# A GNN's first layer taken by chunks, with two of sixteen tiles' source rows by one-hot products from an on-chip table

## The chip, the cores and the metric

The kernel runs on one core of a Trainium2 chip. The core's engines work side by side: TensorE (PE; its weight loads are listed apart as PEld), VectorE (DVE), ScalarE (ACT), GpSimd (POOL) and SyncE (SP), with DMA queues that these engines issue to. The time is that of the device for one execution, in microseconds (us); the smaller, the better. Beside it stands one execution recorded by the profiler, whose span runs from the first to the last recorded event.

## The reference

A graph has N = 12,500 nodes with 32 features each and E = 400,000 edges, sorted by their target node `dst`; the source nodes `src` are random. Four layers follow each other, each on `h = relu(layernorm(x))`, and each adds its result to `x`:

```python
# layer 0
m = relu(h[src] + edge_attr_32)
x = x + (1 + eps) * h + segment_sum(m, dst)
# layer 1: messages from h[src], h[dst] and a 3-vector of the edge, with weights
#          made from edge_attr_10 by a small network; segment_sum over dst
# layer 2: norm * (segment_sum((norm * h)[dst], src) + norm * h), norm = rsqrt(1 + degree of src)
# layer 3: messages from h[src], edge_attr_4 and a network on edge_attr_8; segment_sum over dst
```

Layer 0 is the one whose loop is rewritten. Per edge it fetches a row of 32 numbers by `src`, adds the edge's own 32 numbers, applies relu and sums the result into the row of `dst`. The degree of each node as a source, which layer 2 needs, is counted in the same loop.

## The kernel before

Edges are taken in tiles of 128 (one edge per partition), 3136 tiles in all; 16 tiles are a chunk (196 chunks of 2048 edges) and 4 tiles a group, so a chunk has 4 groups. As `dst` is sorted, the targets of a chunk usually fall into a window of 128 consecutive nodes. `setup()` and `windows()` run ahead of the layers. `setup()` writes zeros to ten tables of 1.56 MB that collect the sums (`acc`, on ACT's DMA queue, L281), loads and scales the weights of the later layers (L126 to L187), and loads `x`. `windows()` loads `dst` (L203), works out each edge's place in its chunk's window (L214) and stores the places for later (`local`, L218; `loc_t`, L225, in another order), decides by a flag (L251) whether all windows fit, and then normalizes the edges' 3-vectors for layer 1 in two orders (L257 to L277, with `rsqrt`, L291 to L296). The flag is read into a register and chooses between two programs; the profile is that of the one for fitting windows, called fast here.

`layer0()` starts with the layer norm of `x` (L309 on), which writes `feat0`, the table of rows that edges fetch. Then `edges()` (L440) runs over chunks and groups. It fetches four groups ahead: on SP the chunk's `src` (L395), its `edge_attr` (L393) and its places (`local`, L376), and on POOL one indirect DMA per tile (L401), which gathers 128 rows of `feat0` by 128 indices into a buffer `hs`. There are six such buffers of one group each (`gather0`), and two of each chunk load (`big0`).

Per group, `main` adds the edge attributes on DVE (L523, 128x128) and applies relu on ACT (L524). `tail`, one group later, calls `collect`: DVE makes four one-hot matrices of the places (L350, 128x512) and TensorE multiplies them with the messages (L353, the one-hot as the weights, 32 columns moving, f32), accumulating the chunk's window in PSUM. After the last group ACT copies the window (`wsum`, L356) and SP writes it to one of two tables in turn (L366). Also in `tail` is the degree: the source number is split into `hi` and `lo` (L538 to L541), both become bf16 one-hots (L545) and TensorE multiplies them (L548); DVE adds the chunk's histogram to the sum (L551).

Nothing orders the work but the program order on each engine, the queues, and the number of buffers in each pool. After the loop the two tables are loaded and added to `x` (`gather_sum`, `part<-acc`). Layers 1 and 2 are fused, layer 3 follows; neither is touched.

Of the kernel before, what the change touches and what calls it, by code (L numbers as in the profile page):

```python
# [8 lines left out]
F32 = mybir.dt.float32  # L9
# [8 lines left out]
D = 32  # L18
# [8 lines left out]
NTAB = 4  # L27
ROUND = 12582912.0
# [7 lines left out]
class GNN:  # L36
# [14 lines left out]
    def __init__(self, tc, ctx, a, out, E):  # L51
# [15 lines left out]

        self.mid = dram.tile([rows, D + 1], F32, name="mid", tag="mid")
# [10 lines left out]
    def setup(self):  # L79
# [18 lines left out]
        once = ExitStack()  # L98
        pool = once.enter_context(self.tc.tile_pool(name="once", bufs=1))
# [9 lines left out]
        nc.vector.tensor_scalar_mul(self.minus, self.part, -1.0)  # L109
        self.eye = keep.tile([P, P], F32, name="eye")  # L110
# [5 lines left out]
        zero = pool.tile([P, J * D], F32, name="zero")  # L116
        nc.vector.memset(zero, 0.0)
        for l in range(4):
            for t in self.tabs[l] if l == 2 else self.tabs[l][:2]:
                self.clear(t, zero)  # L120
            nc.scalar.dma_start(self.feats[l][self.N :], zero[:, :D])
        nc.scalar.dma_start(self.mid[self.N :], zero[:, : D + 1])


        self.w1a = keep.tile([10, 16], F32, name="w1a")
# [4 lines left out]
        self.w2a = keep.tile([16, 896], F32, name="w2a")  # L130
# [8 lines left out]


# [4 lines left out]
        self.w1t = keep.tile([P, P], F32, name="w1tk")  # L145
        nc.vector.tensor_scalar_mul(self.w1t, hid, math.sqrt(2.0) / math.sqrt(10.0))
        lo = pool.tile([P, 6, P], F32, name="wlo")
        hi = pool.tile([P, 4, P], F32, name="whi")
        for r in range(2):
            nc.sync.dma_start(lo[64 * r : 64 * r + 64], self.a["w2lo"])  # L150
            nc.sync.dma_start(hi[64 * r : 64 * r + 64], self.a["w2hi"])
        self.w2t = keep.tile([P, 6, P], F32, name="w2t")
# [5 lines left out]
                                       op0=ALU.mult, op1=ALU.add)  # L158

        mod = pool.tile([P, 8], F32, name="mod")  # L160
        nc.vector.tensor_reduce(mod, self.eye.rearrange("p (k w) -> p w k", w=8), AX.X, ALU.add)
        self.sums = keep.tile([P, 6, D], F32, name="sums")
        nc.vector.memset(self.sums, 0.0)
        for j in range(3):
            nc.vector.tensor_copy(self.sums[:, j, 8 * j : 8 * j + 8], mod)
            nc.vector.tensor_copy(self.sums[:, 3 + j, 0:24].rearrange("p (w i) -> p w i", i=3)[:, :, j], mod)

        self.w1b = keep.tile([8, 256], F32, name="w1b")
        nc.sync.dma_start(self.w1b, self.a["L3_gnn_fc_w1"])
        nc.vector.tensor_scalar_mul(self.w1b, self.w1b, math.sqrt(2.0) / math.sqrt(8.0))  # L170
        self.w1q = keep.tile([P, 256], F32, name="w1q")
# [3 lines left out]
        nc.vector.tensor_scalar_mul(self.w1q, self.w1q, math.sqrt(2.0) / math.sqrt(8.0))  # L175
        rawb = pool.tile([P, 2, 4, 8, 8], F32, name="w2rawb")
        nc.sync.dma_start(rawb.rearrange("p c i w u -> p c (i w u)"),
                          self.a["L3_gnn_fc_w2"].rearrange("(c p) f -> p c f", p=P))
        self.w2b = keep.tile([P, 2, 256], F32, name="w2b")
# [260 lines left out]
    def edges(self, load, gather, front, main, tail, begin=None, windowed=None):  # L440
# [4 lines left out]
        with self.tc.For_i(0, self.T // IT, 1) as it:  # L445
# [22 lines left out]
            for g in range(n):  # L468
# [5 lines left out]
                if g:  # L474
                    tail(*state.pop(g - 1))
# [875 lines left out]
```

## Time and profile before

| what | us |
|---|---|
| median of 3 executions | 23369.61 (23297.51 to 23409.01) |
| the profiled execution, its own time | 23468.87 |
| its span | 23467.2 |
| from the start to the first gather of layer 0 | 388.0 |
| layer 0, first gather to the loading of its tables | 388.0 to 5326.6 |
| layers 1 and 2 | about 5405 to 16,680 |
| layer 3 | about 16,680 to 23,417 |
| POOL's gathers of layer 0 (L401), 3136 of them | 3105.7 busy |

In the page of the profile a row of digits cuts the span into 40 equal slices; a digit is the busy share of an engine in tenths. A group is one line of the source on one engine: the operation, what it writes and reads, its count, then its busy time, the mean duration of one in ns, and how long the engine stood idle just before it, with what ended most of that. "Issue" is idle time that ended by nothing the profile shows; "remote" (in the chain of waits "another core or an unknown queue") is a wait whose releaser the trace could not tie to an instruction of this core. The answers on stretches of time list the busy time and the number of instructions of each engine, the clock that TensorE was granted, the busy share of the DMA engines and the GB/s they moved.

### The profile page before, as it was taken

How to read it: one execution, taken by the hardware profiler on the slowest of the kernel's cores; microseconds unless marked ns; L12 is line 12 of the kernel's file. 1: busy time of each engine (PE TensorE's matmuls, PEld its weight loads, DVE VectorE, ACT ScalarE, POOL GpSimd, SP SyncE). 2: the span in 40 equal slices, each digit the busy share in tenths (PEclk: the TensorE clock that was granted, in tenths of full speed). 3: DMA queues.
4: the chain of work that ended last, by engine and by line, in shares of the span. 5: the costliest groups of instructions: out<-in, count | busy, mean ns of one | idle time of the engine just before them, and what ended most of it. 6: DMA issues, size and time to landing. Idle time of an engine off the chain costs nothing.

```text
span 23467.2 us, 229097 instructions
## 1 busy us (share of the span) xinstructions
PE 15908.4 (68%) x74484; PEld 8469.3 (36%) x74484; DVE 11846.5 (50%) x24268; ACT 5514.0 (23%) x12941; POOL 14360.9 (61%) x12552
## 2 busy tenths in 40 slices
PE   1333333335877787777778777777488888888887
PEld 1333333332333333333333333333254445545444
DVE  4333333334555555555555555556355555555555
ACT  0000000002222222222222222222133333333333
POOL 2666666664777777777777777777444444444443
PEclk9999999998777777777777777777688887788887
DMA  2111111112333333333333333334100000000000
GB/s 97 23 23 22 23 23 23 22 23 64 81 79 80 80 80 78 76 78 80 78 77 82 77 82 77 80 79 80 32 12 12 12 12 12 12 12 12 12 12 18
DMA packets 1486556, 1138.48 MB, mean 49 GB/s; under 512 B 1139620, under 2 KB 1290484, under 8 KB 1430308
## 3 DMA queue, kind: packets, MB, share of 16 engines
q1 hardware_dynamic: 728300, 889.84, 12.3%
q0 software_dynamic: 752640, 206.32, 10.9%
q10 hardware_dynamic: 4398, 27.49, 0.3%
q8 instruction: 591, 9.68, 0.2%
q14 instruction: 627, 5.14, 0.1%
HBM read 1022.56 MB, written 99.86 MB: 48 GB/s over the span
## 4 chain that ended last, share of the span: by engine, by line
PE 38%; DVE 18%; another core or an unknown queue 16%; issue 12%; ACT 9%; POOL 3%; DMA 3%; DVEq 0%; SPq 0%; ACTq 0%; POOLq 0%
PE ps_y L709 10%; PE ps_w L1125 10%; PE ps_o L719 4%; PE ps L842 4%; ACT oh L744 3%; DVE z L712 3%; PE ps_h L1103 2%; DVE pb L1135 2%; ACT oh L673 2%; DVE rb L1143 2%; PE ps_win L353 2%; POOL hs L401 1%; PE ps_sum L1164 1%; DMA hs<-feat,src 1%
## 5 line engine op out<-in xcount | busy, mean ns | idle before, releaser
L848 POOL DMA_INDIRECT acc<-summed,rows x3136 | 4995.2, 1593 | 1969.5 <-issue 1074.5
L1093 POOL DMA_INDIRECT hs<-feat,src x3136 | 3085.5, 984 | 3658.9 <-DVE pb L1135 2663.2
L401 POOL DMA_INDIRECT hs<-feat,src x3136 | 3105.7, 990 | 2196.0 <-issue 873.2
L1125 PE MATMUL ps_w<-w2b,hid 128*128 128x256 f32 x12544 | 4007.2, 462 | 638.0 <-issue 457.3
L667 POOL DMA_INDIRECT hs<-feat,src_c x3136 | 3173.7, 1012 | 1139.1 <-issue 931.3
L353 PE MATMUL ps_win<-m,oh 128*128 128x32 f32 x6272 | 1498.8, 403 | 3077.2 <-ACT m L524 2203.0
L1125 PEld LDWEIGHTS ps_w<-w2b,hid 128*128 128x128 f32 x12544 | 2733.1, 228 | 2327.7 <-issue 1596.3
L712 DVE TENSOR_TENSOR z<-ps_y,hid 128x1024 f32<-128x1024 f32 x2352 | 2843.1, 1218 | 1195.4 <-PE ps_y L709 1006.7
L709 PE MATMUL ps_y<-X,w2t 64*128 64x512 f32 x4704 | 2253.6, 836 | 675.3 <-ACT hid L704 375.8
L353 PEld LDWEIGHTS ps_win<-m,oh 128*128 128x128 f32 x6272 | 1399.8, 328 | 3173.0 <-ACT m L524 2258.9
L1130 DVE TENSOR_TENSOR pa<-ps_w,q 128x512 f32<-128x512 f32 x784 | 540.1, 689 | 3158.9 <-PE ps_w L1125 2902.5
L719 PE MATMUL ps_o<-z,sums 128*32 128x512 f32 x9408 | 1929.8, 695 | 0.9 <-DVE z L712 0.6
L709 PE MATMUL ps_y<-Q,w2t 64*128 64x512 f32 x4704 | 1678.0, 737 | 91.3 <-DVE z L712 40.8
L686 PE MATMUL ps_m<-eye,hs 128*32 128x128 f32 x6272 | 803.1, 367 | 1007.7 <-ACT X L692 780.1
L842 PEld LDWEIGHTS ps<-hd,eq 128*128 128x128 f32 x6272 | 1039.7, 251 | 1229.4 <-issue 324.6
L842 PE MATMUL ps<-hd,eq 128*128 128x32 f32 x6272 | 1135.7, 334 | 508.4 <-DVE eq L834 174.6
L695 DVE TENSOR_TENSOR Q<-N,X 128x512 f32<-128x512 f32 x392 | 272.1, 695 | 2159.7 <-ACT X L692 1359.3
L1105 ACT ACTIVATE hid<-ps_h 128x1024 f32<-128x1024 f32 x784 | 800.1, 1021 | 2177.8 <-PE ps_h L1103 1850.9
L1135 DVE TENSOR_TENSOR pb<-ps_w,hs 128x256 f32<-128x256 f32 x3136 | 1286.5, 476 | 0.0
L709 PEld LDWEIGHTS ps_y<-X,w2t 64*128 64x128 f32 x4704 | 605.5, 238 | 1720.5 <-issue 728.2
L1103 PE MATMUL ps_h<-emb,w1q 8*128 8x512 f32 x3136 | 1067.5, 762 | 228.9 <-DMA emb<-in_ea_c 165.0
L350 DVE TENSOR_TENSOR oh<-iota,local 128x512 f32<-128x512 f32 x784 | 536.9, 685 | 1174.1 <-remote 1033.5
(190 smaller groups left out, 18558.0 us busy)
## 6 DMA issues: line engine op xcount, KB each, us to landing
has<-loc_t SPq DMA_DIRECT2D x392, 1024.0 KB
srow<-in_src_t SPq DMA_DIRECT2D x392, 512.0 KB
hs<-feat,src POOLq DMA_INDIRECT x6272
N<-n_t SPq DMA_DIRECT2D x3136, 32.0 KB
edge_attr<-in_edge_attr SPq DMA_DIRECT2D x196, 256.0 KB
hs<-feat,src_c POOLq DMA_INDIRECT x3136
acc<-summed,rows POOLq DMA_INDIRECT x3136
emb<-in_ea_c SPq DMA_DIRECT2D x784, 20.0 KB
```

Of the source, the lines that this page charges most:

```text
L353: nc.tensor.matmul(c["sum"], lhsT=oh[:, k, :], rhs=feat[:, k, :], start=t0 + k == 0, stop=t0 + k == self.CT - 1)
L401: self.nc.gpsimd.indirect_dma_start(out=t[:, k, :], out_offset=None, in_=self.feats[l][:], in_offset=bass.IndirectOffsetOnAxis(ap=idx[:, t ...
L667: nc.gpsimd.indirect_dma_start(out=c["hs"][:, k, :], out_offset=None, in_=self.feats[1][:], in_offset=bass.IndirectOffsetOnAxis(ap=c["src_ ...
L709: nc.tensor.matmul(y[:, q, :], lhsT=self.w2t[64 * q : 64 * q + 64, j, :], rhs=c["Q" if j < 3 else "X"][64 * q : 64 * q + 64, h, :], start= ...
L712: nc.vector.tensor_mul(z, y, c["hid"][:, 2 * h : 2 * h + 2, :])
L719: nc.tensor.matmul(c["o", j // 3][32 * q : 32 * q + 32, :], lhsT=self.sums[:, j, :], rhs=c["z", j, q // 2][:, q % 2, :], start=j % 3 == 0, ...
L842: nc.tensor.matmul(t[:, k, :], lhsT=c["eq"][:, k, :], rhs=c["hd"][:, G * g + k, :], start=True, stop=True)
L848: nc.gpsimd.indirect_dma_start(out=self.tabs[2][k % NTAB][:], out_offset=bass.IndirectOffsetOnAxis(ap=c["rows"][:, G * g + k : G * g + k + ...
L1093: nc.gpsimd.indirect_dma_start(out=c["hs"][:, k, :], out_offset=None, in_=self.feats[3][:], in_offset=bass.IndirectOffsetOnAxis(ap=c["src" ...
L1103: nc.tensor.matmul(t[:, q, :], lhsT=self.w1q[r : r + 8, m * P : (m + 1) * P], rhs=c["emb"][r : r + 8], start=True, stop=True)
L1125: nc.tensor.matmul(w[:, k, :], lhsT=c["hid"][:, m, 4 * g + k].rearrange("p q s -> p (q s)"), rhs=self.w2b[:, m, :], start=m == 0, stop=m == 1)
L1135: nc.vector.tensor_mul(c["pb"][:, i, gs], w[:, :, lo : lo + 64].rearrange("p g (w u) -> p g w u", u=8), by[:, :, None, :].to_broadcast([P, ...
```

## The change

The loop of layer 0 is replaced for the fast program by `edges0`, which works on whole chunks. Three things differ in it.

First, from the fourth chunk on, POOL gathers only 14 of the 16 tiles. The rows of the last two tiles (256 edges) are looked up on chip. `table` loads `feat0` once as 3157 rows of 4 nodes (the table has 128 spare rows), in 25 blocks of up to 128 such rows, and splits each number into three bf16 parts that add up to it. `codes`, run once, writes for each of the 256 edges of each chunk three numbers: the block, the place in the block and which of the four nodes. SP loads them to all 128 partitions. `found` compares the place with the partition number (`mine`), then for each of 25 blocks makes a bf16 one-hot (DVE, 128x256) and has TensorE multiply three parts of the table with it, 75 products summed in one PSUM tile: column e then holds the four nodes' 128 numbers of edge e's row. A mask keeps the node that is meant (`own`), a product with `fold` turns and sums it, and ACT copies the result beside the gathered rows.

Second, the one-hots of the window sums are made by ACT (16 Square and 4 Relu per chunk, `places`), and `collect` uses the messages as 32-column weights in four column tiles; `add` folds the four parts together one chunk later. The message sum and its relu run once per chunk (128x512), as do the coordinates of the degree.

Third, the setup is shorter: the norm of layer 0 stands ahead of `windows()`, `dst` is loaded on ACT's queue, and clearing tables, the weights, `loc_t` and the normalized vectors move into a generator, `rest`. Two of its steps (the clearing of layer 0's own two tables) are taken ahead of the loop, the others inside it, two per group from the fifth chunk on: 10 clears, 6 for weights, 8 for places, 84 for the vectors, now in 14 blocks. The program for windows that do not fit keeps the old loop (`any0`).

```diff
--- before.py
+++ after.py
+KP = 2
+KB = 25
...
     def setup(self):
...
-        for l in range(4):
-            for t in self.tabs[l] if l == 2 else self.tabs[l][:2]:
-                self.clear(t, zero)
...
+    def weights(self, pool):
...
+    def rest(self, pool):
+        nc, J = self.nc, self.J
+        zero = pool.tile([P, J * D // 8], F32, name="zero")
+        nc.vector.memset(zero, 0.0)
+        for l in range(4):
+            for t in self.tabs[l][:2] if self.fast and l != 2 else self.tabs[l]:
+                self.clear(t, zero)
+                yield
+        yield from self.weights(pool)
+        if self.fast:
+            yield from self.places_by_edge(pool)
+            yield from self.unit_vectors(pool)
...
     def windows(self):
...
-            nc.sync.dma_start(dst.rearrange("p w t -> p (w t)"), self.a["dst"])
+            nc.scalar.dma_start(dst.rearrange("p w t -> p (w t)"), self.a["dst"])
...
-        with self.tc.tile_pool(name="unit", bufs=1) as pool:
...
+    def places_by_edge(self, pool):
...
+    def unit_vectors(self, pool):
+        nc, F = self.nc, self.T // 14
...
     def clear(self, t, zero):
-        self.nc.scalar.dma_start(self.nodes(t[: self.N]), zero[:NP])
+        self.nc.scalar.dma_start(self.nodes(t[: self.N]).rearrange("p (k e) -> p k e", k=8),
+                                 zero[:NP, None, :].to_broadcast([NP, 8, zero.shape[1]]))
...
     def layer0(self):
-        self.norm_relu(0)
...
+            if self.fast:
+                rest = self.rest(ctx.enter_context(tc.tile_pool(name="rest", bufs=1)))
+                for _ in range(2):
+                    next(rest)
+                self.edges0(rest)
...
+    def codes(self):
+        nc, half, n = self.nc, self.NW // 2, KP * P
+        with self.tc.tile_pool(name="codes", bufs=1) as pool:
+            s = pool.tile([half, 2, n], I32, name="s")
+            rows = self.a["src_t"].rearrange("(c h t) e -> c h t e", h=2, t=self.CT)[:, :, self.CT - KP :, :]
+            for h in range(2):
+                nc.sync.dma_start(s[:, h].rearrange("c (t e) -> c t e", e=P), rows[:, h])
+            code = pool.tile([half, 2, 3, n], F32, name="code")
+            row = pool.tile([half, 2, n], F32, name="row")
+            block, place, node = (code[:, :, i] for i in range(3))
+            for t, k in ((block, 512.0), (row, 4.0)):
+                nc.vector.tensor_scalar(t, s, -0.5 * (k - 1.0), 1.0 / k, op0=ALU.add, op1=ALU.mult)
+                nc.vector.tensor_scalar_add(t, t, ROUND)
+                nc.vector.tensor_scalar_add(t, t, -ROUND)
+            nc.vector.scalar_tensor_tensor(place, block, -128.0, row, op0=ALU.mult, op1=ALU.add)
+            nc.vector.scalar_tensor_tensor(node, row, -4.0, s, op0=ALU.mult, op1=ALU.add)
+            nc.vector.tensor_scalar_add(block, block, 1.0)
+            nc.sync.dma_start(self.code.rearrange("(c h) i e -> c (h i e)", h=2), code.rearrange("c h i e -> c (h i e)"))
+    def table(self, pool, l):
+        nc = self.nc
+        tab = pool.tile([P, 3, KB, P], BF16, name="tab")
+        with self.tc.tile_pool(name="whole", bufs=1) as tmp:
+            x = tmp.tile([P, KB, P], F32, name="whole")
+            rows = self.feats[l].rearrange("(r k) d -> r (k d)", k=4)
+            n = rows.shape[0] // P
+            nc.vector.memset(x[:, n:, :], 0.0)
+            nc.sync.dma_start(x[:, :n, :], rows[: n * P].rearrange("(b p) e -> p b e", p=P))
+            nc.sync.dma_start(x[: rows.shape[0] - n * P, n, :], rows[n * P :])
+            for k in range(3):
+                nc.scalar.copy(tab[:, k], x)
+                if k < 2:
+                    nc.vector.tensor_tensor(x, x, tab[:, k], op=ALU.subtract)
+        return tab
+    def edges0(self, rest):
+        nc, tc, CT, NW = self.nc, self.tc, self.CT, self.NW
+        n = KP * P
+        FIRST = 3
+        self.codes()
+        with ExitStack() as ctx:
+            tp = ctx.enter_context(tc.tile_pool(name="table0", bufs=1))
+            tab = self.table(tp, 0)
+            ld = ctx.enter_context(tc.tile_pool(name="load0", bufs=4))
+            wp = ctx.enter_context(tc.tile_pool(name="work0", bufs=2))
+            ps = ctx.enter_context(tc.tile_pool(name="ps0", bufs=2, space=PSUM))
+            pt = ctx.enter_context(tc.tile_pool(name="pt0", bufs=1, space=PSUM))
+            def fetch(c):
+                c["src"] = self.load(ld, "src", c["col"])
+                c["attr"] = self.load(ld, "edge_attr_32", c["col"])
+                c.update(self.places_of(ld, c["no"]))
+                if c["no"] >= FIRST:
+                    c["code"] = ld.tile([P, 3, n], F32, name="code", bufs=2)
+                    nc.sync.dma_start(c["code"].rearrange("p i e -> p (i e)"),
+                                      self.code[c["no"] : c["no"] + 1].rearrange("o i e -> (o i e)").partition_broadcast(P))
+                c["hs"] = ld.tile([P, CT, D], F32, name="hs")
+                for k in range(CT if c["no"] < FIRST else CT - KP):
+                    nc.gpsimd.indirect_dma_start(
+                        out=c["hs"][:, k, :], out_offset=None, in_=self.feats[0][:],
+                        in_offset=bass.IndirectOffsetOnAxis(ap=c["src"][:, k : k + 1], axis=0))
+            def found(c, step):
+                if c["no"] < FIRST:
+                    return
+                if step == 0:
+                    c["mine"] = wp.tile([P, n], BF16, name="mine")
+                    nc.vector.scalar_tensor_tensor(c["mine"], c["code"][:, 1], self.part, c["code"][:, 0],
+                                                   op0=ALU.is_equal, op1=ALU.mult)
+                    c["rows4"] = pt.tile([P, n], F32, name="ps_rows")
+                elif step < 6:
+                    oh = wp.tile([P, 5, n], BF16, name="oh4")
+                    for k in range(5):
+                        b = 5 * (step - 1) + k
+                        nc.vector.tensor_scalar(oh[:, k], c["mine"], float(b + 1), None, op0=ALU.is_equal)
+                    for k in range(5):
+                        b = 5 * (step - 1) + k
+                        for i in range(3):
+                            nc.tensor.matmul(c["rows4"], lhsT=tab[:, i, b], rhs=oh[:, k],
+                                             start=(b, i) == (0, 0), stop=(b, i) == (KB - 1, 2))
+                else:
+                    own = wp.tile([P, n], F32, name="own")
+                    nc.vector.scalar_tensor_tensor(own, c["code"][:, 2], self.quad, c["rows4"],
+                                                   op0=ALU.is_equal, op1=ALU.mult)
+                    t = pt.tile([P, KP, D], F32, name="ps_own")
+                    for k in range(KP):
+                        nc.tensor.matmul(t[:, k, :], lhsT=own[:, k * P : (k + 1) * P], rhs=self.fold, start=True, stop=True)
+                    nc.scalar.copy(c["hs"][:, CT - KP :, :], t)
+            def messages(c):
+                m = c["m"] = wp.tile([P, CT, D], F32, name="m")
+                nc.vector.tensor_add(m, c["hs"], c["attr"])
+                nc.scalar.activation(m, m, AF.Relu)
+            def places(c, g):
+                oh = c["oh", g] = wp.tile([P, G, P], F32, name="oh")
+                for k in range(G):
+                    t = G * g + k
+                    nc.scalar.activation(oh[:, k, :], self.iota, AF.Square, bias=c["local"][:, t : t + 1], scale=-1.0)
+                nc.scalar.activation(oh, oh, AF.Relu, bias=self.one, scale=-2.0)
+            def collect(c, g):
+                if g == 0:
+                    c["sum"] = ps.tile([P, B], F32, name="ps_sum")
+                for k in range(G * g, G * g + G):
+                    j = 32 * (k % 4)
+                    nc.tensor.matmul(c["sum"][j : j + 32, 0:P], lhsT=c["m"][:, k, :], rhs=c["oh", g][:, k % G, :],
+                                     start=k < 4, stop=k >= CT - 4)
+            def add(c):
+                s4 = wp.tile([P, P], F32, name="s4")
+                nc.scalar.copy(s4, c["sum"][:, 0:P])
+                nc.tensor.matmul(c["sum"][:, P : P + D], lhsT=s4, rhs=self.fold, start=True, stop=True)
+                s = wp.tile([P, D], F32, name="wsum")
+                nc.scalar.copy(s, c["sum"][:, P : P + D])
+                self.put(0, c, s)
+            cs = [{"no": c, "col": c * CT} for c in range(NW)]
+            for c in range(2):
+                fetch(cs[c])
+            for c in range(NW + 1):
+                now, last, next_ = (cs[k] if 0 <= k < NW else None for k in (c, c - 1, c + 1))
+                if c + 2 < NW:
+                    fetch(cs[c + 2])
+                for g in range(CG):
+                    if now:
+                        if g == 0:
+                            messages(now)
+                            now["deg"] = ps.tile([P, P], F32, name="ps_deg")
+                            now["hl"] = self.coordinates(wp, now["src"])
+                        places(now, g)
+                        hi, lo = now["hl"]
+                        self.degree(wp, now, hi[:, G * g : G * g + G], lo[:, G * g : G * g + G], G * g)
+                    if next_:
+                        for step in ((0, 1), (2, 3), (4, 5), (6,))[g]:
+                            found(next_, step)
+                    if now:
+                        collect(now, g)
+                    if last and g == 0:
+                        add(last)
+                    for _ in range(2 if c > 3 else 0):
+                        next(rest, None)
+            for _ in rest:
+                pass
...
         g.setup()
+        g.norm_relu(0)
         ok = g.windows()
```

`weights` holds the loads and scalings that stood in `setup`, with a `yield` after each; `places_by_edge` and `unit_vectors` hold what stood in `windows`, in blocks. `coordinates` and `degree` are the lines L538 to L551 of before as functions; `gather`, `put` and `places_of` are as before.

## The prediction

> **What bounds the kernel now.** I read the slices of the page first, to split the span into stages, then the groups, then windows by stage, then the waits and the timeline inside layer 0, the only layer that the change rewrites.
>
> The page, its slices and two of its groups (busy us, mean ns; then idle before, and what ended most of it):
>
> ```profile
> PE   1333333335877787777778777777488888888887
> POOL 2666666664777777777777777777444444444443
> L401 POOL DMA_INDIRECT hs<-feat,src x3136 | 3105.7, 990 | 2196.0 <-issue 873.2
> L353 PE MATMUL ps_win<-m,oh 128*128 128x32 f32 x6272 | 1498.8, 403 | 3077.2 <-ACT m L524 2203.0
> ```
>
> The windows before the first gather, of layer 0, and of layers 1 and 2 (length, busy us of PE, PEld, DVE, ACT, POOL, clock, DMA share, GB/s):
>
> ```profile
> 0.00:388.00 388.00, 1.82 (x4) 1.00 (x4) 180.53 (x124) 24.48 (x45) 0.91 (x8) 1.00 0.35 135
> 388.00:5327.00 4939.00, 1821.54 (x9408) 1726.30 (x9408) 1821.18 (x6461) 271.73 (x980) 3105.68 (x3136) 1.00 0.13 23
> 5405.00:16680.00 11275.00, 8670.09 (x42730) 3399.93 (x42730) 6278.92 (x12169) 2948.10 (x6821) 8167.32 (x6271) 0.76 0.38 78
> ```
>
> Layer 0 takes 4939 us for 196 chunks, 25.2 us each. No engine is full: POOL 63%, PE and DVE 37%, ACT 5%. A gather costs 0.990 + 873.2/3136 = 1.268 us on POOL, and 16 of them 20.3 us. The other 4.8 us a chunk are POOL's waits: 2196.0 − 873.2 of issue − 386 of setup = 937 us, over 196. Who makes POOL wait? The waits of layer 0 (us in total, times, longest):
>
> ```profile
> ACT wsum L356 <- remote: 1470.9, 81, 22.5
> DVE oh L350 <- remote: 944.6, 110, 19.7
> POOL hs L401 <- DVE oh L350: 506.1, 51, 15.6
> POOL hs L401 <- DMA src<-in_src: 235.8, 30, 15.3
> ```
>
> and one such wait in the timeline (start, duration, then the idle time before):
>
> ```profile
> 2496.71 0.64 PE L548 MATMUL ps_deg<-olo,ohi 128*125 128x100 bf16 x4
> ...
> 2512.12 0.94 POOL L401 DMA_INDIRECT hs<-feat,src  x1 [0.30 <-issue]
> 2516.33 0.19 ACT L356 COPY wsum<-ps_win 128x32 f32<-128x32 f32 x1 [21.40 <-remote]
> 2516.33 0.69 DVE L350 TENSOR_TENSOR oh<-iota,local 128x512 f32<-128x512 f32 x1 [12.69 <-remote]
> ...
> 2521.88 1.44 POOL L401 DMA_INDIRECT hs<-feat,src  x1 [8.82 <-DVE m L523]
> ```
>
> TensorE's last matmuls of that chunk are recorded at 2496.7, but the engines that wait for them go on at 2516.3, about 3 us after POOL has filled its six gather buffers and stopped. So every second chunk loses some 9 us: gathers of about 41 us, then a pause. Gathers bound layer 0, plus these late completions, whose nature the trace doesn't tell.
>
> **What the Trainium skill says.** "Perfetto Trace Analysis", section "DMA Instruction — SWDGE (GPSIMD)": such a record ends when descriptors are generated, not when data have moved. The trace agrees: gathers follow each other every 1.25 us while the DMA share is 0.13; only fewer gathers shorten POOL's time. "TensorE: Matmul & The Clock Gate", Part 1: the array runs at half clock until some 3.4 us of activity, and falls back after idling. The trace agrees in the later layers (0.76 granted in layers 1 and 2); for layer 0, the 1.00 isn't supported by any clock event before 5447 us, and its sparse matmuls come at half rate. "TensorEngine Tiling (Array Packing)", section "Available Configurations": four 128×32 column tiles run at once, as layers 1 and 2 here do already; section "Key Properties" adds that switching between tilings drains the array, which the new loop does some eight times a chunk. The trace shows no price for it; the rows of layers 1 and 2 that follow such a switch come within 0.1 us, so I take nothing, and at most 8 × 0.2 us, which the idle part of TensorE hides.
>
> **The change, part by part, per chunk.**
> POOL: 14 gathers, 14 × 1.268 = 17.75 us. With busier engines beside it a gather of layers 1 and 2 took 1012 ns (L667), so 14 × 1.31 = 18.4. I take 18.2.
>
> TensorE gains 75 bf16 matmuls of 256 columns, not shown before. The skill's price ("TensorE: Matmul & The Clock Gate", section "Back-to-back issue gap") is N/2.4 + 2.5 ns warm and N/1.2 cold: 0.109 and 0.213 us, so 8.2 or 16.0 us. Sixteen degree matmuls 1.2 or 2.2 (four took 0.55 us), sixteen collects in column tiles 0.9 or 1.7, two own-row products 0.6 or 0.9, the fold 0.25 or 0.5. Sum 11.2 us warm, 21.3 cold; waits at the seams between chunks (messages to one-hots to collect) bring the cold one to about 24. These are estimates. Warm, 11.2 hides under 18.2; at the layers' 0.76 to 0.80 clock, about 15, also hidden. I take warm to mixed: a cold array would be busy without pause, and that is what the skill says warms it.
>
> VectorE loses four one-hots of 0.69, four 128×128 sums of 0.29 and three of four rounds of coordinates (4 × 0.16 each): 2.7 + 1.2 + 1.9. It gains one 128×512 sum, 0.69, twenty-five bf16 comparisons of 128×256 and two small passes. The nearest rows are 0.16 (128×4) and 0.29 (128×256 f32), so 25 × 0.07 to 0.15 = 1.7 to 3.8, plus 0.8. From 11.6 to about 10 us: hidden. If they cost the whole 0.29, 13.5, still hidden.
>
> ScalarE gains 16 Square of 0.31 (as m L524), four Relu of 128×512 at 0.71, two copies: about 9 us against 1.4. Hidden, but the copy of the looked-up rows waits for TensorE and stands ahead of the chunk's relu and wsum, which so depend on TensorE's count.
>
> SP's queue gains the code load, 393 KB a chunk; with attributes and gathers 880 KB in 18.2 us is 48 GB/s, where layers 1 and 2 move 78. Hidden. SP's order per chunk stays ahead of the gathers: loads are issued two chunks early.
>
> Buffers: there are four of a whole chunk where there were six of a quarter. The gathers of chunk c + 2 wait for the message sum of chunk c − 2 on VectorE, with two whole chunks gathered between, so lateness up to about 2 × 18 = 36 us is covered; the lateness before was 20. The 4.8 us of pauses go. Without this cover they cost 9 us in two chunks, 22.5 a chunk.
>
> **Ahead of the loop.** Of the 388 us before the first gather, table clearing up to 142, the weights, and the unit vectors from 179.7 to 347 leave the path. What stays: x and its norm, 35; dst now on ACT's queue, landing at about 44; places and flag 24 (179.5 − 156.0), 68; the branch and the 1.6 MB table load 17, 85; three ACT copies of 2.86 and two subtractions of 3.49, 15.6, 101; the first src loads, which reuse that memory, and the first gather: about 112. The first three chunks still gather all 16: 48 × 1.29 = 62.
>
> The removed setup work comes back in chunks 4 to 17. A block of unit vectors is 672 elements in four passes, 448 in a reciprocal (19.75 × 448/3136 = 2.8) and four more passes, and 672 in two: 9.3 us of VectorE, fourteen times. At eight steps a chunk that is 12 us more on VectorE, 22 against 18.2: 4 × 10.5 chunks = 44; with table loads of 1.28 on ACT I take +50. Fully hidden it is 0, not hidden at all 130.
>
> **Sum** for layer 0's end: 112 + 62 + 193 × 18.2 + 50 + 20 for the drain = 3757 us, against 5327: 1570 less. Later layers are unchanged. The profiled execution took 23468.9, its span 23467.2, so 21,897 of span; the median shown is 0.42% lower, 23369.6 − 1570 = 21,800.
>
> **Rivals.**
> Even better (chance 0.09): POOL runs at its floor, 17.3 us a chunk, the moved work is hidden, and two 40 us waits at the start of layers 1 and 2 go as well: 3514 − 60, about 21,500.
> TensorE becomes the bound (0.19): it stays at half clock, about 24 us a chunk: 112 + 62 + 193 × 24 + 70 = 4876, 451 less, 22,920. For it: layer 0's cold rate now, and a granted clock of 0.76 to 0.80 even in the dense layers. Against: 75 unbroken matmuls.
> Slower (0.12): completions on TensorE become visible only when POOL's stream stops. That hardly mattered with a pause every 41 us. Now the looked-up rows themselves need TensorE, so each period is two chunks of gathers, 35.5 us, and then two chunks of TensorE, 2 × 11 to 2 × 21: 29 to 39, about 34 us a chunk, 6806 at the end of layer 0, 24,850. It decides from 25.2 + 276/196 = 26.6 us a chunk. For it: the timeline above. Against: in layers 1 and 2 POOL streams for over 100 us and TensorE's completions are at most some 12 us late.
> The forecast has 0.60; its own range, 17.7 to 19.3 us a chunk and 0 to 130 for the moved work, is 21,550 to 22,100.
>
> **Range and chances.** 21,450 to 22,950 takes in all but the slower case. A measurement can tell about 0.5%, 117 us. Faster 0.86, the same 0.02, slower 0.12.
>
> **What would show it.** First gather near 112; gathers of a steady chunk 14 in 17.5 to 18.5 us without pauses above 3 us; VectorE over 90% busy for some ten chunks after 200 us; layer 0's last put near 3750; PE busy near 62% of layer 0; the later layers unchanged within 50 us. I am wrong if ACT's copy of the looked-up rows waits over 10 us and POOL stops behind it (TensorE late or cold), if gathers lengthen above 1.1 us beside VectorE's bf16 passes, or if the moved work holds POOL for hundreds of us.

## The result, and the profile after

The changed kernel took 23433.94 us (median of 20; 23352.01 to 23508.61) against 23385.43 (20 runs of the kernel before beside it): a ratio of 1.0018, with an interval of 1.0005 to 1.0031. The forecast was 21,800. Chips differ in what follows: on some the kernel before takes 23,385 to 23,857 us, on others 19,322 to 19,368, and each run below is compared with the kernel before on its own chip. The first four runs and those on the chip of 23,857 us are of a single execution each.

The page after, its slices and the groups of the new loop (columns as before):

```profile
PE   3676666666788777877887777777488888888887
POOL 4555555554777777777777777777444444444443
PEclk7777677667777777777777777777688878888787
L679 POOL DMA_INDIRECT hs<-feat,src x2750 | 2706.4, 984 | 2563.8 <-DVE m L713 1530.6
L700 PE MATMUL ps_rows<-oh,tab 128*128 128x256 bf16 x14475 | 2483.7, 327 | 1282.8 <-issue 1055.2
```

POOL works less than before in layer 0 (fives where sixes were), and its main wait is now for the message sum on VectorE. The answers on the gathers' line say where the layer ends (min/median/max ns, first and last start), and those on a steady stretch count its chunks by the copies of `wsum`, one per chunk:

```profile
L679 POOL DMA_INDIRECT hs<-feat,src x2750: 938/944/5870, 142.2 to 5271.1; - x197
```

```profile
1000.00:5000.00 4000.00, 2772.84 (x19728) 1792.42 (x19728) 1633.31 (x6265) 1335.22 (x3672) 2081.93 (x2140) 0.70 0.15 36
```

```profile
1000.00:5000.00 4000.00, 28.33 (x153) 0.70 0.15 36
```

The second fence is of all engines, the third of `wsum` alone. The kernel before, its gathers' line and its copies of `wsum`:

```profile
L401 POOL DMA_INDIRECT hs<-feat,src x3136: 939/947/1876, 388.0 to 5302.6; - x196
1000.00:5000.00 4000.00, 29.59 (x159) 1.00 0.13 23
```

A chunk takes 4000/153 = 26.1 us; before it took 4000/159 = 25.2. So the first gather comes 246 us earlier (142.2 for 388.0) and the loop gives nearly all of it back: the last gather is at 5271.1, before at 5302.6. The waits in the stretch from 1000 to 5000 us, after:

```profile
ACT oh L720 <- remote: 1966.6, 193, 14.5
PEld L700 <- issue: 1415.7, 1296, 4.6
POOL hs L679 <- DVE m L713: 1312.3, 153, 10.8
...
PE ps_rows L700 <- issue: 888.8, 976, 5.1
```

POOL waits 1312.3/153 = 8.6 us a chunk for its full buffers, and TensorE idles by "issue", for no reason that the profile shows. The timeline of TensorE in one chunk, whose gathers ran from 2506.39 to 2524.45:

```profile
2509.83 3.44 PE L700 MATMUL ps_rows<-oh,tab 128*128 128x256 bf16 x30
...
2516.48 0.49 PE L700 MATMUL ps_rows<-oh,tab 128*128 128x256 bf16 x3 [0.23 <-issue]
2518.31 1.64 PE L700 MATMUL ps_rows<-oh,tab 128*128 128x256 bf16 x9 [1.34 <-issue]
2520.78 0.80 PE L700 MATMUL ps_rows<-oh,tab 128*128 128x256 bf16 x3 [0.83 <-issue]
2522.18 0.80 PE L700 MATMUL ps_rows<-oh,tab 128*128 128x256 bf16 x3 [0.60 <-issue]
2524.32 0.37 PE L728 MATMUL ps_sum<-oh,m 128*32 128x128 f32 x1 [1.33 <-issue]
2525.03 0.37 PE L728 MATMUL ps_sum<-oh,m 128*32 128x128 f32 x1 [0.34 <-issue]
2526.45 0.69 PE L728 MATMUL ps_sum<-oh,m 128*32 128x128 f32 x6 [1.04 <-issue]
```

First thirty products in 3.4 us, the estimated 0.11 each. Then twos, threes and nines with gaps, and restarts 0.7 or 1.4 us apart; the last six matmuls start 2 us after the last gather has ended. I call this creeping. Some of the gaps pass through VectorE: the nine at 2518.31 need comparisons that VectorE began at 2517.96, after waiting for TensorE. Half clock isn't what slows it first: from 2515 to 2518 us the granted clock was 1.00, and 8 matmuls started in these 3 us, where 36 had started from 2509 to 2512. Nor is it one chunk's accident. Over the 165 stretches of gathers between 900 and 5200 us, matmul records per us, by the time since the stretch began (worked out from the trace's records; in the median a stretch is 17.6 us long, a pause 8.2):

```
since start, us    0-3  3-6  6-9  9-12  12-15  15-18  18-21  21-24
matmuls per us     8.3  9.9  4.6   2.1    1.3    1.6    2.6    6.2
```

And of 17,747 matmuls that wait for no semaphore, 468 start over 0.6 us after their own weight load, 379 of them by 0.6 to 0.8 us and 52 by 1.3 to 1.4, none in the first 3 us of a stretch. Such gaps stand in the trace of the kernel before too, in layer 3, from 12 to 26 us after its gathers begin, where I had not looked.

Layer 3, which no run below changes, thus tells in every trace what kind of chip it met. Of some 21,950 matmuls there that wait for no semaphore, 1315 to 1383 start over 0.6 us after their weight load in the traces of chips where the kernel before takes 23,385 us or more, and 8 in the traces of the others (counted from the trace's records).

### The profile page after: what moved, and what is told of

Read it like the earlier page. It is cut to its first block, busy times and chain, and to the rows that moved or that the text cites. A ratio compares the mean times of both kernels' runs of the same rounds, so it can differ in the third digit from the quotient of the medians.

```text
span 23361.9 us, 266381 instructions
## 1 busy us (share of the span) xinstructions
PE 17583.0 (75%) x90123; PEld 9018.7 (39%) x90123; DVE 12110.4 (52%) x25907; ACT 6958.1 (30%) x16678; POOL 13964.9 (60%) x12166
## 4 chain that ended last, share of the span: by engine, by line
PE 49%; DVE 17%; issue 11%; another core or an unknown queue 10%; ACT 9%; DMA 1%; POOL 1%; DVEq 0%; ACTq 0%; SPq 0%; POOLq 0%
PE ps_y L914 10%; PE ps_w L1330 10%; PE ps_rows L700 9%; PE ps_o L924 4%; PE ps L1047 4%; ACT oh L949 3%; DVE z L917 3%; DVE rb L1348 3%; DVE pb L1340 2%; PE ps_h L1308 2%; PE ps_sum L728 2%; ACT oh L878 2%; PE ps_deg L570 2%; PE ps_sum L1369 1%
## 5 line engine op out<-in xcount | busy, mean ns | idle before, releaser
L1298 POOL DMA_INDIRECT hs<-feat,src x3136 | 3083.3, 983 | 3642.8 <-DVE pb L1340 2647.9
L679 POOL DMA_INDIRECT hs<-feat,src x2750 | 2706.4, 984 | 2563.8 <-DVE m L713 1530.6
L700 PE MATMUL ps_rows<-oh,tab 128*128 128x256 bf16 x14475 | 2483.7, 327 | 1282.8 <-issue 1055.2
L700 PEld LDWEIGHTS <-tab 128*128 128x128 bf16 x14475 | 1604.5, 114 | 2029.1 <-issue 1680.5
L720 ACT ACTIVATE oh<-iota,local 128x128 f32<-128x128 f32 x3136 | 1052.6, 392 | 2844.2 <-remote 2384.7
L696 DVE TENSOR_SCALAR oh<-mine 128x256 bf16<-128x256 bf16 x4825 | 796.6, 237 | 2081.4 <-remote 1193.8
L1049 ACT COPY summed<-ps 128x128 f32<-128x128 f32 x784 | 207.8, 265 | 3627.1 <-PE ps L1047 2199.9
```

The source lines that it names most:

```text
L679: nc.gpsimd.indirect_dma_start(out=c["hs"][:, k, :], out_offset=None, in_=self.feats[0][:], in_offset=bass.IndirectOffsetOnAxis(ap=c["src" ...
L700: nc.tensor.matmul(c["rows4"], lhsT=tab[:, i, b], rhs=oh[:, k], start=(b, i) == (0, 0), stop=(b, i) == (KB - 1, 2))
L720: nc.scalar.activation(oh[:, k, :], self.iota, AF.Square, bias=c["local"][:, t : t + 1], scale=-1.0)
L1298: nc.gpsimd.indirect_dma_start(out=c["hs"][:, k, :], out_offset=None, in_=self.feats[3][:], in_offset=bass.IndirectOffsetOnAxis(ap=c["src" ...
```

## The experiments

Theory A: the stream of gathers slows TensorE, from some 9 us into an unbroken stretch until some 3 us after it has ended. Theory B, the prediction's rival: half clock and the seams of its program hold TensorE, whatever POOL does.

### On a chip without creeping: what each part costs alone

The first four runs met such a chip (kernel before: 19,330 us). They tell the costs, not yet the cause. Runs that leave out gathers or products leave out a part of the sums, as their expectations say.

**Four gathers.**

```diff
-                for k in range(CT if c["no"] < FIRST else CT - KP):
+                for k in range(CT if c["no"] < FIRST else 4):
...
-                nc.vector.tensor_add(m, c["hs"], c["attr"])
...
+                    nc.vector.tensor_add(m[:, :4], c["hs"][:, :4], c["attr"][:, :4])
+                    nc.vector.tensor_copy(m[:, 4 : CT - KP], c["attr"][:, 4 : CT - KP])
+                    nc.vector.tensor_add(m[:, CT - KP :], c["hs"][:, CT - KP :], c["attr"][:, CT - KP :])
```

> The changed kernel with 4 instead of 14 gathers per chunk from the fourth chunk on; the other ten tiles' messages take the edge attributes alone, so that part of the sum is left out. Theory A (the stream of gathers slows TensorE: from about 9 us into a stretch of unbroken gathers its instructions come in steps of 0.7 us, until some 3 us after the stretch): a stretch is now 5 us long and never gets there, TensorE runs at its own pace, 12 to 15 us a chunk instead of 25.8, the whole about 21,100 (20,800 to 21,500). Theory B (TensorE's own work at half clock, with its seams, is the bound, whatever POOL does): 24 to 26 us a chunk, the whole 23,200 to 23,500.

17,593 us. From 1000 to 2200 us there are 99 chunks, 12.1 us each, and TensorE is busy throughout (500.00 of 500 us in one stretch) at a granted clock of 1.00: that is its own pace, near the 11.2 us of the forecast's sum.

**No products.** `found` returns at once, and the code isn't loaded.

> The changed kernel without the lookup: 14 gathers per chunk, no comparisons, no table products, no code loads in the loop; the last two tiles' messages take the edge attributes alone. Theory A: TensorE has 34 short matmuls left; if it creeps by 0.7 us while gathers stream, these cost it up to 20 us, so 18 to 22 us a chunk, the whole 21,800 to 22,700. Theory B: TensorE has 5 us of work, POOL's 14 gathers bound the chunk at 17.8, the whole 21,800. If the chunk stays at 25 as before the change, neither is right.

18,671 us, 18.3 us a chunk: POOL's 14 gathers, as both said.

**All gathers.** `FIRST = NW`, without `codes` and `table`.

> The changed kernel with all 16 tiles gathered in every chunk and neither table nor lookup: the short setup, the sums in column tiles and the one-hots on ScalarE alone. Both theories: POOL's 16 gathers, 20.3 us, bound the chunk unless TensorE creeps; 20.5 us a chunk gives about 22,350. Theory A allows up to 25 us, 23,200, if the creeping still holds up the sums; theory B doesn't.

19,077 against 19,330, 20.4 us a chunk: 16 gathers, without a pause. The first gather comes at 68.4 us instead of 388.0, and the total is 253 us less. That the difference goes to the setup work inside the loop is likely, but isn't shown: the kernel before wasn't profiled on such a chip.

**Rows by plain DMA.**

```diff
-                    nc.gpsimd.indirect_dma_start(
-                        out=c["hs"][:, k, :], out_offset=None, in_=self.feats[0][:],
-                        in_offset=bass.IndirectOffsetOnAxis(ap=c["src"][:, k : k + 1], axis=0))
...
+                        r = P * ((c["no"] * CT + k) % 97)
+                        nc.sync.dma_start(c["hs"][:, k, :], self.feats[0][r : r + P, :])
```

> The changed kernel with the 14 gathers of a chunk replaced by 14 plain DMAs on SP's queue, each of 128 contiguous rows (wrong rows, same 128 pieces of 128 bytes): the same data moved, but POOL idle. Theory A in the form that POOL's making of descriptors slows TensorE: 12 to 15 us a chunk, the whole about 21,100. Theory A in the form that the transfers themselves slow it: above 20 us, 22,300 to 23,400. Theory B: 24 to 26, 23,200 to 23,500.

17,585 us, 12.1 us a chunk, TensorE full again.

### On chips with creeping

**The changed kernel, and all gathers, again.**

> The changed kernel as it is, on the same chip as a run of the kernel before. The four runs so far met a chip on which the kernel before took 19,330 us instead of 23,385, and in which TensorE never fell to half clock or crept in layer 0 of the first of them (12.1 us a chunk). Theory A and the prediction's own chunk then say: where TensorE keeps its pace, 14 gathers bound the chunk at 17.8 us, about 18,700 against 19,330 (a ratio near 0.967); where it creeps, the ratio stays at 1.00 and the kernel before stands near 23,385. Theory B: 24 to 26 us a chunk on either chip, which would be slower than the kernel before on the faster one, above 19,900.

> The changed kernel with all 16 tiles gathered and no lookup, measured for a ratio. Where TensorE keeps its pace: 16 gathers, 20.3 us a chunk, about 19,080 against 19,330, a ratio near 0.987. Where it creeps: theory A says that little work is left for it to be late with, but window sums may still be, 20.5 to 25 us a chunk, 22,350 to 23,200 against 23,385.

On this chip the kernel before took 23,466 us, the changed one 23,451 (ratio 0.9987, interval 0.9973 to 1.0000, 26.0 us a chunk). With all 16 gathered and no lookup it took 23,181: 0.9875 (0.9843 to 0.9907), 24.8 us a chunk. The short setup is the gain there (the gathers run from 68.5 to 4967.8 us, as long as the kernel before's 388.0 to 5302.6), and the lookup takes it away again. The chunk with little TensorE work has not come down to the 20.4 us of the other chip: in the median POOL still goes 41 us and pauses 9.4, as before the change (41 and 8.9). But neither in this layer 0 nor in that of the kernel before does any matmul that waits for no semaphore start over 0.6 us after its weight load. What is late there are completions, as in the prediction's timeline. As the pauses are missing on the other chip (none over 3 us from 900 us on in the run with all gathers), one cause for both is likely; no run shows it.

**Four gathers, plain DMAs, fills, and pauses,** on a chip where the kernel before took 23,857 us. The changed kernel itself didn't run there; that the chip creeps shows in layer 3 of these four runs (1315 to 1369 late matmuls in each). The edits of the first two are those above. In the third each gather is replaced by `nc.gpsimd.memset(c["junk"], 0.0)` of 128x1024. The fourth:

```diff
...
                     nc.gpsimd.indirect_dma_start(
...
+                    if c["no"] >= FIRST and k % 7 == 6:
+                        for _ in range(4):
+                            nc.gpsimd.memset(junk, 0.0)
```

> Four gathers instead of 14 per chunk once more (the other ten tiles' messages are the edge attributes alone), for a chip on which TensorE creeps (kernel before near 23,400). Theory A: stretches of 5 us of gathers don't reach the creeping, so TensorE runs at its own pace, 12 to 15 us a chunk in layer 0, total near 21,000. Theory B: the creeping is TensorE's own in this program, 22 to 26 us a chunk, total above 22,800. On a chip without creeping (before near 19,330): 12.1 us a chunk, as measured.

> Plain DMAs on SP's queue in place of the gathers once more (wrong rows, the same pieces). On a chip with creeping: if POOL's making of descriptors slows TensorE, no creeping, 12 to 15 us a chunk; if the transfers of small pieces do, creeping as with gathers, 20 to 26 us. On a chip without: 12.1 us, as measured.

> The gathers replaced by 14 fills of a 128x1024 buffer on POOL (the gathered rows are left out, the messages of these tiles take the buffer's zeros): POOL busy, no descriptors, no transfers. On a chip with creeping: if being busy on POOL is enough to slow TensorE, gaps of 0.7 us between its instructions and over 20 us a chunk; if it takes descriptors or transfers, none, and the chunk is the longer of TensorE's 12 to 15 us and 14 fills.

> The changed kernel, with POOL spending four fills of a 128x1024 buffer after every seventh gather, so that no stretch of gathers is longer than 8.8 us. Theory A: nearly no gaps of 0.7 us are left in TensorE's stream, and the chunk is what POOL takes: 17.6 us plus eight fills, 22 to 26 by the length of a fill; POOL becomes the bound, without pauses for full buffers. Theory B: TensorE's gaps and its 25.8 us stay as they are.

Totals: 21,365, 21,140, 22,005 and 23,456 us. Steady stretches of layer 0 (all engines), in this order:

```profile
1000.00:2600.00 1600.00, 1495.37 (x15487) 1173.91 (x15485) 1200.84 (x5161) 1038.09 (x2881) 466.28 (x481) 1.00 0.23 58
```

```profile
1000.00:2400.00 1400.00, 1400.00 (x14921) 1126.75 (x14919) 1181.20 (x4736) 1001.17 (x2778) 0.00 (x0) 1.00 0.35 78
```

```profile
1000.00:3200.00 2200.00, 1764.16 (x16908) 1356.78 (x16906) 2101.80 (x5565) 1076.88 (x3035) 1745.87 (x1752) 0.91 0.15 42
```

```profile
1000.00:4800.00 3800.00, 2413.33 (x20548) 1795.46 (x20547) 2604.21 (x6556) 1345.46 (x3751) 3315.50 (x3414) 0.80 0.18 39
```

By the copies of `wsum` (120 in 1600 us, 116 in 1400, 127 in 2200 and 149 in 3600) these are 13.3, 12.1, 17.3 and 24.2 us a chunk. The same TensorE program that took 26 us takes 12 to 13, at full clock, when POOL's gathers are few or plain DMAs stand in their place: theory B falls. (With fills VectorE is the busiest engine, 2101.80 of 2200 us.) Of the matmuls that wait for no semaphore none starts more than 0.6 us after its weights in any of the four runs. Fills keep POOL busier than the gathers did (1746 of 2200 us), and TensorE doesn't creep; plain DMAs bring as many rows, and it doesn't. What is left is what only the gathers have: transfers that POOL prepares and that go through its queue, or rows at scattered addresses. No run tells these apart, since the plain DMAs went through SP's queue and took contiguous rows.

In the run with pauses, the order of work put the fills singly between gathers, not in two blocks (POOL's timeline):

```profile
2512.56 1.28 POOL L680 DMA_INDIRECT hs<-feat,src  x1 [0.30 <-issue]
2514.15 0.94 POOL L680 DMA_INDIRECT hs<-feat,src  x1 [0.30 <-issue]
2515.40 0.94 POOL L680 DMA_INDIRECT hs<-feat,src  x1 [0.30 <-issue]
2516.33 0.98 POOL L685 MEMSET junk<- 128x1024 f32 x1
2517.47 0.95 POOL L680 DMA_INDIRECT hs<-feat,src  x1 [0.16 <-issue]
```

Still no creeping with all 14 gathers, at one gather in 24.2/14 = 1.73 us, never more than four in a row and breaks of about 1 us between. With eight fills of nothing in every chunk this kernel took 0.983 of the one before, in one pair of executions, too few for a verdict.

### How much of a break is needed

**Short and longer fills, and the kernel before with fills.** A `memset` of 128x128 or 128x384 after every gather of the changed kernel, of 128x256 after every gather of the old one.

> The changed kernel with a fill of a 128x128 buffer on POOL after every gather from the fourth chunk on; nothing is left out. In the run with pauses POOL did not take its fills in two blocks after seven gathers: they came one by one between gathers, at most five gathers stood together, the gaps of 0.7 us in TensorE's stream were gone, and the chunk took 23.75 us, all of it POOL's. Theory A1 (any other work between gathers is enough): no gaps, 14 gathers at 1.25 plus 14 short steps, 18 to 20 us a chunk, about 1,150 to 1,500 us less than the changed kernel on a chip with creeping, a ratio of 0.935 to 0.955. Theory A2 (it takes time without descriptors, as much as 0.8 us): gaps as before, near 26 us a chunk, a ratio of 1.00. On a chip without creeping: 0.97 to 0.98.

> The same with fills of 128x384, three times as long (0.36 us by the 0.96 of a 128x1024 one). A1: no gaps, and 14 times 0.2 us or so more than with short fills, 20 to 22.5 us a chunk, a ratio of 0.95 to 0.97. A2: if the short fills leave some gaps, these leave fewer, and the chunk is shorter than with the short ones in spite of the longer fills.

> The kernel before the change, with a fill of 128x256 after every gather of layer 0. Theory A says that its 20 us late completions are the same creeping: they go, POOL no longer pauses for full buffers, and the chunk is 16 gathers with their fills, 20.5 to 22.5 us instead of 25.2: 500 to 900 us less, a ratio of 0.96 to 0.98. If the late completions have another cause: pauses stay, 25 us or more, a ratio of 1.00 to 1.02. On a chip without creeping the fills only cost: 1.00 to 1.02.

> The changed kernel as it is, beside the runs with fills. On a chip with creeping a ratio of 0.998 to 1.002. On a chip without (before near 19,330), where it has not run yet: 17.8 to 18.3 us a chunk and a ratio near 0.967.

These met a chip without creeping (kernel before: 19,368), so the question stayed open. The fills only cost there: ratios of 1.0078, 1.0099 and 1.0341 (1.0320 to 1.0361), and the short ones, not tied to any gather, were bunched by the order of work. But the fourth run is the forecast's own case. It took 18,800, a ratio of 0.9705 (0.9685 to 0.9724). Its gathers' line, all engines in a steady stretch, and the copies of `wsum` in it:

```profile
L679 POOL DMA_INDIRECT hs<-feat,src x2750: 943/947/5608, 142.8 to 3868.9; - x197
```

```profile
1000.00:3400.00 2400.00, 1821.04 (x16487) 1363.83 (x16488) 1339.01 (x5244) 1106.24 (x3068) 1854.57 (x1790) 0.85 0.23 50
```

```profile
1000.00:3400.00 2400.00, 23.81 (x128) 0.85 0.23 50
```

18.75 us a chunk, where the forecast had 18.2, and the last gather at 3869 instead of 5271. The same 2750 gathers have a median of 947 ns here and of 944 on the other chip, so the 1402 us between the chips are not POOL's work. Here POOL bounds the chunk: it is busy 1854.57 of the 2400 us and idles 521.3 more by "issue" between gathers. TensorE is partly at half clock here too (0.85), and it doesn't matter.

**A forced fill before every fourth gather.**

```diff
...
+                    if c["no"] >= FIRST and k % 4 == 0:
+                        nc.gpsimd.memset(c["hs"][:, k : last, :], 0.0)
                     nc.gpsimd.indirect_dma_start(
```

> The changed kernel with POOL filling the rest of the chunk's gather buffer (448, 320, 192, 64 elements wide) before every fourth gather, which the gathers then overwrite, so that the order is forced and at most four gathers follow each other. Nothing is left out. On a chip with creeping, if a break of 0.1 to 0.5 us every 5 us is enough: no gaps of 0.7 us, 14 gathers at 1.25 to 1.31 and 1.2 us of fills, 18.5 to 20 us a chunk instead of 26, a ratio of 0.94 to 0.955 against the kernel before. If the break has to be longer or come after every gather: gaps stay, above 23 us a chunk, a ratio of 0.98 to 1.00. On a chip without creeping: the changed kernel's 0.970 plus 1.2 us a chunk, 0.98.

> The kernel before with a fill of 128x256 after every gather of layer 0, for a chip with creeping. On the chip without it POOL took 1.49 us for a gather and its fill, 23.9 us a chunk, with no pauses. If the late completions are the creeping: 23.9 us here too, no pauses for full buffers, 250 us less than the kernel before, a ratio of 0.99. If they have another cause: pauses stay on top, 28 us, a ratio of 1.02 or more.

Again a chip without creeping: 0.9784 (0.9767 to 0.9800) and 1.0328. The kernel before with fills takes 24.1 us a chunk (measured in its first run): POOL's 1.50 us for a gather and its fill. What the fills do to its late completions was not learnt, since neither run met a creeping chip.

> A fill before every fourth gather once more, for a chip with creeping (kernel before near 23,400 to 23,900). If a break of 0.1 to 0.5 us every 5 us is enough: no gaps of 0.7 us in TensorE's stream in layer 0, 18.5 to 20 us a chunk, a ratio of 0.94 to 0.955. If not: gaps stay, above 23 us a chunk, 0.98 to 1.00. On a chip without creeping: 0.978, as measured.

This one met one (kernel before: 23,846): 23,794, a ratio of 0.9977 (0.9962 to 0.9991). All engines, then `wsum`:

```profile
1000.00:5000.00 4000.00, 2834.56 (x19743) 1802.71 (x19742) 1641.93 (x6276) 1337.53 (x3672) 2271.55 (x2756) 0.72 0.17 36
```

```profile
1000.00:5000.00 4000.00, 28.32 (x153) 0.72 0.17 36
```

26.1 us a chunk, and 559 of the long gaps against 468: breaks of 0.4 to 0.75 us every 5 us are of no use. One gather in 18.1/14 = 1.29 us with these breaks creeps, one in 1.73 with breaks of 1 us doesn't.

> The changed kernel with a fill of 128x384 after every gather once more, for a chip with creeping. So far on such chips: a gather every 1.25 us creeps, 14 gathers in 18.1 us (1.29 each) with a break of at most 0.75 us every fourth creep as well, a fill of 0.96 us after most gathers (1.70 each) does not. Here a gather comes every 1.55 us. If the rate or a break of 0.6 us after each gather is enough: no gaps of 0.7 us, 21.7 to 22.6 us a chunk set by POOL, a ratio of 0.96 to 0.975. If not: gaps stay, 24 to 28 us a chunk, 0.99 to 1.02. On a chip without creeping: 1.010, as measured.

A chip without creeping once more (1.0105, interval 1.0076 to 1.0135). Where between the two the limit lies, and whether the rate of the gathers or the length of the break sets it, is open.

## Why the prediction was wrong

**The step that failed** is TensorE's line in the sum: "Warm, 11.2 hides under 18.2 ... I take warm to mixed". Its estimate of TensorE's own pace was near (12.1 us measured with TensorE full, on either kind of chip), but on the chip of the forecast TensorE delivers these 12 us of work in 26, because it creeps while gathers stream. The prediction put that loss at nothing in its sum and left it to a rival of 0.12. The step on buffers failed with it: "lateness up to about 36 us is covered". In this loop it was no lateness of fixed size that buffers can bridge but a loss of pace, from 9.9 matmuls a us to 1.3 in the table above, and the 75 products fell into the very stretch where TensorE creeps. The prediction's own sign of being wrong came close: ScalarE waited 1966.6 us in 193 waits, 10.2 us each, though before its one-hots and not at the copy of the looked-up rows.

**The rivals.** The slower one named the right thing, that TensorE suffers while POOL streams, and priced it at 34 us a chunk against 26.1, because it took all of TensorE's time in a stretch as lost; in fact the first 9 us of a stretch and the pause are good. It set its point of decision at 26.6, so the measured chunk is a draw, as was the total. The argument that gave it only 0.12 was the mistake: that in layers 1 and 2 TensorE's completions are at most 12 us late says nothing on its pace. Layer 3 of the trace before had the 0.7 us gaps. The half-clock rival gave 24 us, near the measured value for the wrong reason: the granted clock falls to 0.70 in that loop, but TensorE slows before the clock does (8 matmuls in 3 us at 1.00, above), and the clock was 0.85 where the chunk took 18.75.

**The other steps.** POOL's chunk: 18.2 forecast, 18.75 where POOL bounds it; a gather took 1050 ns on average in that run, not 990. First gather: 142 for 112; VectorE's subtractions for the table stood behind weights and places that the order of work had moved ahead of the loop, so that the table was ready at 124.6, not 101, and SP's first src loads came at 135. VectorE: 1633/153 = 10.7 us a chunk for 10; but it rose rather than fell, since the prediction's 11.6 for the kernel before adds up passes that overlap, where its own table has 1821.18/196 = 9.3 busy. ScalarE: 8.7 for 9. The moved work: +50 forecast; on the chip without creeping POOL issued 355 gathers from 300 to 800 us against 373 to 376 in the stretches after, some 25 us; VectorE was busy 77% there (61% on the chip of the forecast), not over 90%. Later layers: 5399.8 to 16221.8 for the gathers of layers 1 and 2, against 5402.3 to 16305.2: 81 us less, within 1% but beyond the 50 us named. Three slips of the prediction change nothing: 25 comparisons at 0.29 give VectorE 14.5 us, not 13.5; the low end of the forecast's own range is about 21,650 by its terms, not 21,550; and the first clock event lies at 5437 us, not 5447.

**The size.** Where TensorE keeps its pace the changed kernel saves 568 us by the two medians, not 1570: the kernel before has no late completions to lose there, if its 16 gathers run as in the run with all gathers (20.4 us a chunk, no pauses). That is argued; its own layer 0 wasn't profiled on such a chip.

## What to carry to other kernels

Moving work from a busy engine to an idle one is paid at the idle engine's pace beside the busy one, which need not be its pace alone: look in the trace for how the receiving engine runs just when the giving engine streams, by the time since the stretch began. A wait for "issue" inside a run of ready instructions, or a completion that comes only when another engine stops, is a sign that the two are not independent, and a rival built on it deserves more than a small chance. And measure on more than one chip before saying what a change is worth: this one is 1.00 on one kind and 0.97 on the other.

## What was not expected of the hardware

TensorE, on some chips, falls from 8 to 10 matmuls a us to 1 to 2 after 9 us of gathers at one per 1.25 us, in steps of 0.7 us, and recovers some 3 us after they stop; on others not at all, with the same program (0 gaps of over 0.6 us among 14,362 against 468 among 17,747). The kernel as a whole takes a quarter more on one kind (spans of 23,362 and 18,792 us in two profiled runs of the changed one). Layer 3, also a loop of gathers beside dense matmuls, takes 6627 us from its first to its last gather on the one and 4298 on the other. Its matmuls show the same late starts on the one kind alone (1380 against 8 in these two traces), and its gathers come in stretches of 20 us with pauses on the one (192 pauses over 3 us) and without a pause on the other. Whether all of the difference is the same creeping no run here shows, as no run changed layer 3. Nor do the runs show what in the chips differs.
